# Kernel3 of a Nystrom attention block: two passes of scores with tokens on partitions instead of one pass and transposes

## The chip, the cores and the metric

The kernel runs on one core of a Trainium2 chip. The metric is device time of one execution in microseconds (us). The core has a matrix engine (TensorE, in the profile PE, with its weight loads as PEld), a vector engine (DVE), a scalar engine (ACT), a general engine (POOL) and a queue for transfers (SP). PE writes its products to PSUM; the other engines read them from there.

## The reference

The input `x` is 16 batches of 1024 tokens by 256 features. A block of attention and a block of experts follow each other, each on normalized input, each added to its input after a second normalization. The attention, cut to what matters:

```python
H, M = (16, 64)                      # heads, landmarks; HD = 16
Q = Q / HD ** 0.5
Q_l = Q.reshape(b, H, M, n // M, HD).mean(axis=-2)     # one landmark for 16 tokens
K_l = K.reshape(b, H, M, n // M, HD).mean(axis=-2)
kernel1 = softmax(einsum('bhnd,bhmd->bhnm', Q, K_l), axis=-1)
kernel2 = softmax(einsum('bhmd,bhkd->bhmk', Q_l, K_l), axis=-1)
kernel3 = softmax(einsum('bhmd,bhnd->bhmn', Q_l, K), axis=-1)
SV = matmul(matmul(kernel1, iterative_inv(kernel2)), matmul(kernel3, V))
out = transpose(SV, (0, 2, 1, 3)).reshape(b, n, c) @ w_proj
```

`iterative_inv` is six rounds of four 64x64 products for each head. The second block computes eight expert reconstructions of every token, takes for each batch the expert of least loss, gathers that expert's adapter weights by its number, and adds the adapter's output to a base product. The change concerns `kernel3` and its product with `V` alone: for each head, 64 landmarks against 1024 tokens, a softmax over the tokens, and a sum of V over the tokens with these weights.

## The kernel before

All data is float32. Each batch passes four stages: `stage_a` (normalize, transpose, Q, K, V, landmarks, kernel3 and its product with V, called `u`), `stage_p` (kernel2 and its inverse, then the inverse times `u`, called `pw`), `stage_c` (kernel1, its product with `w_bd`, the projection) and `stage_d1`/`stage_d2` (experts, choice, gather, adapter). Four streams run through the batches at once, so that in the steady part PE works on stage a of one batch, p of the batch before and c and d of the ones before these. In the trace of batch 8's stage a, stage p works on batch 7, c on 6 and d on 5.

The order of instructions on PE, ACT, DVE and POOL is written out by the program. Every stage is a generator that yields a `go(name, follows, parts)` ahead of each piece of work: the parts are planned durations on the engines (`mm` for PE, with the mode of the array and the pool of PSUM; `ew` for the others), and a planner at the end of the file chooses the stream whose next piece can start first on PE, with its own clocks and its own model of the PSUM buffers. Engines then run their instructions strictly in that order. PSUM is one pool, `ps2`, of four buffers of two banks; every product tile takes the next of the four in turn, and must wait until the tile that had it before is read.

Kernel3 in stage a works in four steps, two groups of 8 heads (`c`) by two halves of 512 tokens (`n`):

- `scores` (L339 to L352): four products of 32 rows each (`psc`, landmarks of two heads on the 128 partitions, 512 tokens in the free direction) in two PSUM tiles; DVE takes the negated maximum of each row (`nmx`, L349), and ACT the exponential with that as bias and the row's sum as a second output (`e`, L352).
- `turned` (L368, L370): sixteen 128x128 transposes of `e`, so that tokens stand on partitions, and two copies by ACT back to SBUF (`e3t`).
- `times_v` (L379, L386): sixteen products, for each of four token blocks and four pairs of heads, with 32 columns of `v` as the stationary operand, and a copy (`ut`).

At the end the two halves, which have different maxima, are brought together (`share`, L430 to L438), four transposes turn `ut` back (`pu`, L443), and DVE scales and adds (`un`, `u`, L448 and L452).

Stage c does kernel1 in two passes: maxima first (`max_of`, L648 and L656), transposed to rows (L677, L679), then scores with a second product that subtracts the maximum (`weights`, L686 and L694, exponential L704), then products with 34 columns of `w_bd`, 17 for each head, of which the last is a column of ones that gives the sum (`weighted`, L715 to L726). Stage p's products are L491, with ACT's copies `kv` (L571), `sq` (L586), `vi` and `vt` (L609, L611) and DVE's `t1` (L574), `t2` (L584), `t3` (L595). Stage d has the hidden products `ph` (L833), the reconstructions `pr` (L865), DVE's difference (L873) and ACT's squares (L876), the choice of the expert (`row`, L905 to L914), five gathers by POOL (L917), and the output products `pad` (L945) and `pf` (L960, L961).

## Time and profile before

| what | value |
|---|---|
| median of 11 runs | 2829.7 us (2825.94 to 2833.56) |
| profiled execution, its own time | 2823.92 us |
| its span, first to last instruction | 2822.1 us |
| mean granted clock of TensorE | 0.922 |
| ACT: squares `df` (L876), exponentials `e` of kernel3 (L352), `e3t` copies (L370), exponentials of kernel1 (L704) | 362.8, 172.5, 125.1, 124.2 us busy |
| DVE: `df` (L873), maxima of kernel3 (L349), maxima of kernel1 (L656) | 299.6, 150.2, 149.4 us busy |
| PE: `pr` (L865), `ph` (L833), `pq` (L285), scores of kernel3 (L339) | 253.6, 239.4, 233.0, 76.5 us busy |
| time of the chain that ended last, by engine | PE 62%, DVE 16%, ACT 15%, issue 4% |

Busy time of a group is the union of its instructions' times. A float32 matmul is two matmul records and two weight loads in the trace, a transpose one of each. Matmuls overlap each other, so the time a group of them takes is better read from the start of the group to the start of the next one than from the sum of their durations. "Idle before" is time in which the engine stood still ahead of an instruction, with the instruction that ended the wait; "issue" stands where no semaphore explains it. In the list of groups the columns after the count are busy time in us, mean duration in ns, and idle time before in us with its releasers.

### The profile page before, as it was taken

The page shows a single profiled execution, that of the slowest core. Times are in us where ns is not written, and L with a number is a line of the kernel's source. Part 1 is how long each engine was busy: PE and PEld are TensorE (multiplying, and loading weights), DVE is VectorE, ACT ScalarE, POOL GpSimd, SP SyncE. Part 2 cuts the span into 40 slices and gives each one's busy share as a digit, 9 for nine tenths or more (in the row PEclk, how much of TensorE's full clock was granted, in tenths as well). Part 3 has the DMA queues.
Part 4 walks back from the last instruction along what each step waited for, and adds up shares of the span by engine and source line. Part 5 has one row for each costly group of instructions (what it writes and reads, how often), then busy time and mean ns, then how long its engine had stood idle before and what let it go on. Part 6 is the DMA issues. An engine that isn't in the chain of part 4 may idle for free.

```text
span 2822.1 us, 86591 instructions
## 1 busy us (share of the span) xinstructions
PE 2400.4 (85%) x39362; PEld 1597.8 (57%) x39362; DVE 1533.6 (54%) x3195; ACT 1396.7 (49%) x2707; POOL 419.9 (15%) x434
## 2 busy tenths in 40 slices
PE   6898979989798898988879888898888979887865
PEld 3566555655656556565565555656566555655542
DVE  4556545465554655546554564555546555464644
ACT  3555644545455463544635545354464545544434
POOL 0001020120301202011120211203012030111131
PEclk9999989989899898998989999898998989999988
DMA  3000010010100101001010010101001010010100
GB/s 94 17 17 18 2 34 17 4 46 2 33 17 4 46 2 34 17 4 46 4 32 17 12 39 4 32 17 30 20 4 46 2 34 2 4 32 4 32 18 17
DMA packets 56569, 60.38 MB, mean 21 GB/s; under 512 B 4949, under 2 KB 55178, under 8 KB 56202
## 3 DMA queue, kind: packets, MB, share of 16 engines
q1 hardware_dynamic: 50176, 50.34, 5.7%
q8 instruction: 309, 5.06, 0.7%
q0 software_dynamic: 2560, 2.14, 0.3%
q10 hardware_dynamic: 3466, 2.37, 0.3%
q14 instruction: 58, 0.48, 0.1%
HBM read 38.06 MB, written 16.78 MB: 19 GB/s over the span
## 4 chain that ended last, share of the span: by engine, by line
PE 62%; DVE 16%; ACT 15%; issue 4%; another core or an unknown queue 1%; ACTq 0%; DMA 0%; POOLq 0%; DVEq 0%; POOL 0%
PE pq L285 8%; PE ph L833 8%; PE pr L865 5%; ACT df L876 5%; ACT e L352 4%; PE pf L960 4%; PE pv L306 4%; PE pt L368 3%; DVE maxima L656 3%; PE pvi L491 3%; PE pkv L491 3%; PE put L379 2%; PE psv L715 2%; PE po L763 2%; DVE nmx L349 2%
## 5 line engine op out<-in xcount | busy, mean ns | idle before, releaser
L876 ACT ACTIVATE df<-df,bd_sb 128x512 f32<-128x512 f32 x512 | 362.8, 711 | 152.7 <-DVE df L873 152.7
L873 DVE TENSOR_TENSOR df<-pr,xt_d 128x1024 f32<-128x1024 f32 x256 | 299.6, 1217 | 104.3 <-PE pr L865 81.8
L352 ACT ACTIVATE e<-psc,nmx 128x512 f32<-128x512 f32 x256 | 172.5, 686 | 207.6 <-DVE nmx L349 175.9
L865 PE MATMUL pr<-ht,wd_sb 64*128 64x512 f32 x1024 | 253.6, 614 | 10.6 <-DVE maxima L656 5.2
L833 PE MATMUL ph<-xt_d,wd_sb 128*128 128x512 f32 x512 | 239.4, 610 | 2.1 <-DVE df L873 1.4
L198 POOL TENSOR_SCALAR ve_c_y<-mv_c_y 128x4 f32<-128x4 f32 x32 | 7.4, 230 | 1557.3 <-DVE mv_c_y L196 1497.3
L285 PE MATMUL pq<-xt_a,wqkv_sb 128*128 128x512 f32 x512 | 233.0, 600 | 0.0
L574 DVE SCALAR_TENSOR_TENSOR t<-pkv,eye 128x512 f32<-128x512 f32 x96 | 65.4, 682 | 221.3 <-ACT kv L571 221.3
L704 ACT ACTIVATE e<-psct 128x1024 f32<-128x1024 f32 x128 | 124.2, 1024 | 96.9 <-PE psct L694 96.9
L656 DVE TENSOR_REDUCE maxima<-psc 128x16 f32<-128x1024 f32 x128 | 149.4, 1218 | 36.2 <-PE psc L648 36.1
L491 PE MATMUL pkv<-vi,k2t 64*64 64x64 f32 x6144 | 125.4, 235 | 49.1 <-ACT vi L609 40.4
L285 PEld LDWEIGHTS pq<-xt_a,wqkv_sb 128*128 128x128 f32 x512 | 95.0, 191 | 116.9 <-issue 112.9
L491 PEld LDWEIGHTS pkv<-vi,k2t 64*64 64x64 f32 x6144 | 110.5, 147 | 88.3 <-ACT vi L609 45.7
L349 DVE TENSOR_REDUCE nmx<-psc 128x2 f32<-128x1024 f32 x128 | 150.2, 1214 | 17.6 <-PE psc L339 17.1
L833 PEld LDWEIGHTS ph<-xt_d,wd_sb 128*128 128x128 f32 x512 | 93.2, 192 | 113.7 <-issue 102.6
L368 PE MATMUL pt<-ident,e 128*128 128x128 f32 x1024 | 143.3, 298 | 11.8 <-ACT e L352 5.8
L865 PEld LDWEIGHTS pr<-ht,wd_sb 64*128 64x128 f32 x1024 | 88.3, 186 | 102.4 <-issue 58.7
L370 ACT COPY e3t<-pt 128x1024 f32<-128x1024 f32 x128 | 125.1, 1023 | 41.2 <-PE pt L368 40.9
L368 PEld LDWEIGHTS pt<-ident,e 128*128 128x128 f32 x1024 | 126.8, 154 | 21.1 <-ACT e L352 8.5
L960 PE MATMUL pf<-wbase_sb,xt_d 128*128 128x256 f32 x512 | 133.2, 382 | 0.0
L195 DVE BATCH_NORM_STATS2 st_d_y<-y_d 128x6 f32<-128x256 f32 x128 | 51.5, 403 | 148.9 <-ACT y_d L239 148.9
L648 PE MATMUL psc<-bd,qt 32*128 32x128 f32 x2048 | 95.6, 324 | 42.1 <-ACT e L352 38.1
(166 smaller groups left out, 4567.4 us busy)
## 6 DMA issues: line engine op xcount, KB each, us to landing
xa<-in_L_attn_x_dram SPq DMA_DIRECT2D x16, 1024.0 KB, 5.5
x<-in_L_attn_x_dram SPq DMA_DIRECT2D x16, 1024.0 KB, 7.6
out_dram<-y_d SPq DMA_DIRECT2D x32, 512.0 KB, 2.9
wqkv_sb<-in_L_attn_w_qkv_dram ACTq DMA_DIRECT2D x1, 768.0 KB, 6.4
wd_sb<-in_L_ffn_Wd_dram ACTq DMA_DIRECT2D x2, 256.0 KB, 12.8
wd_sb<-in_L_ffn_Wd_dram ACTq DMA_DIRECT2D x1, 512.0 KB, 14.1
wdn<-in_L_ffn_Wa_down_dram,row POOLq DMA_INDIRECT x32
wproj_sb<-in_L_attn_w_proj_dram ACTq DMA_DIRECT2D x1, 256.0 KB
```

The costliest lines, as they stand in the source:

```text
L285: nc.tensor.matmul(pq[:, n, :], lhsT=wqkv_sb[:, k, f0 : f0 + P], rhs=xt[:, k, n * 512 : (n + 1) * 512], start=(k == 0), stop=(k == NC - 1),)
L349: nc.vector.tensor_reduce(nmx[:, n, q : q + 2], psc[g], X, ALU.max, negate=True)
L352: nc.scalar.activation(e3[:, i, :], psc[g][:, i, :], AF.Exp, bias=nmx[:, n, q + i : q + i + 1], accum_out=s3[:, n, q + i : q + i + 1],)
L368: nc.tensor.transpose(pt[:, t, i, :], e3s[g][:, i, t * P : (t + 1) * P], ident)
L370: nc.scalar.copy(e3t, pt)
L491: nc.tensor.matmul(dst[64 * h[to] : 64 * h[to] + 64, 4 * h[frm] + 2 * g0 + g1, :], lhsT=x[rows, i, :], rhs=y[rows, j, :] if y_at else y[ro ...
L656: nc.vector.tensor_reduce(mx[:, t0 : t0 + 2, 64 * g : 64 * g + 64].rearrange("x t (p j) -> x p t j", p=2)[:, :, :, 0 : 2 * NC], psc[g].rea ...
L833: nc.tensor.matmul(ph[:, n, :], lhsT=wd1_sb[:, k, 2 * i : 2 * i + 2, :].rearrange("p e h -> p (e h)"), rhs=xt[:, k, n * 512 : (n + 1) * 51 ...
L865: nc.tensor.matmul(pr[:, r, :], lhsT=wd2_sb[half, i, k * P : (k + 1) * P], rhs=ht[half, cols], start=True, stop=True,)
L873: nc.vector.tensor_tensor(df, pr, middle(xt[:, k, cols], 2), ALU.subtract)
L876: nc.scalar.activation(df[:, r, :], df[:, r, :], AF.Square, bias=bd2_sb[:, e, k : k + 1], accum_out=part[:, e, k * NW + n : k * NW + n + 1],)
L960: nc.tensor.matmul(po[:, j, :], lhsT=xt[:, k, cols], rhs=wbase_sb[:, k, :], start=(k == 0), stop=False)
```

## The change

Kernel3 takes the form that kernel1 has, with its sides exchanged. In a first pass the same score products as before are made for all four steps (`max_of`, new L360), and DVE takes only their maxima. The maxima of the two halves are joined (`maxima3`), transposed by one PE transpose (`pm`), and multiplied with a picking matrix into `mrow`, which holds the negative maxima as rows. The second pass (`weights`) has four steps of 256 tokens: four products of `ones` with `mrow` put the negative maximum in every place of a PSUM tile, sixteen products of 128 tokens of `kt` (stationary) with `bd` add the scores, now with tokens on partitions, and ACT takes one exponential over 1024 columns, without bias or sum. `times_v` multiplies these weights, 32 landmarks at a time, with 34 columns of `v_ones`: V with a column of ones beside the 16 of each head, so that the sum over the tokens comes out of the same product. 64 such products of 128 tokens by 32 by 34 make one step; the steps are added in `sums` by one ACT copy and three DVE additions, and at the end DVE divides. The transposes of `e`, the `e3t` copies, `share`, `pu` and `un` are gone. ACT's copy of V now writes into `v_ones` with a gap of one column for each head; the ones are set once by POOL. The planned durations and the order follow: all four steps of the first pass are yielded ahead of the second pass, and the next batch's normalization is yielded after the second step of it. In the changed order of batch 8's neighbourhood, PE has `pr` x4, `pkv3`, three steps of maxima, `psq3`, `psct`, `pb3`, the fourth step of maxima, `psv`, `pvi3`, `psct`, `pkv4`, the transpose of the maxima, `psv`, `psq4`, and then the weights, with `pad`, `pf` and stage p's products between them; the last two V groups stand side by side.

```diff
--- before.py
+++ after.py
@@ -161,6 +161,14 @@
 
 
 
+
+    v_ones = const.tile([P, NT, H, HD + 1], F32, name="v_ones")
+    nc.gpsimd.memset(v_ones.rearrange("p t h d -> p (t h d)"), 1.0)
+
+    maxima3 = const.tile([P, 4, 32], F32, name="maxima3")
+    nc.gpsimd.memset(maxima3, 0.0)
+    minus_pick = const.tile([P, NC], F32, name="minus_pick")
+    nc.vector.tensor_reduce(minus_pick, ident.rearrange("x (p j) -> x j p", j=32)[:, 0:NC, :], X, ALU.add, negate=True)
     w_bds = [const.tile([P, NP, 2, HD + 1], F32, name=f"w_bd{i}") for i in range(2)]
     maxima = [const.tile([P, 4, P], F32, name=f"maxima{i}") for i in range(2)]
     for t in (*w_bds, *maxima):
@@ -262,7 +270,6 @@
             load(b + 1, "xa", 1)
         both = [("a", b, "xt", h) for h in range(NW)]
         qt = kt = None
-        v = work.tile([P, NT, D], F32, tag="v", name=f"v_{b}", bufs=1)
         lsum = small.tile([P, 2, NC, M], F32, tag="lsum", name=f"lsum_{b}", bufs=1)
         for i, scale in enumerate((HD**-0.5, 1.0)):
             for c in range(NC):
@@ -310,7 +317,9 @@
                         start=(k == 0),
                         stop=(k == NC - 1),
                     )
-            nc.scalar.copy(v[:, t0 : t0 + 4, :], pv)
+            nc.scalar.copy(
+                v_ones[:, t0 : t0 + 4, :, 0:HD], pv.rearrange("p j (h d) -> p j h d", d=HD)
+            )
             if t0 == 0:
                 yield go(
                     ("a", b, "bd"),
...
+        mx3 = small.tile([P, NW, NP], F32, tag="mx3", name=f"mx3_{b}")
+        sums = small.tile([P, NP, 2 * (HD + 1)], F32, tag="sums3", name=f"sums3_{b}", bufs=1)
+        TC = 2
+        steps = range(NT // TC)
+
+        def before_max(c, n):
+            return go(
+                ("a", b, "max", c, n),
+                [("a", b, "bd"), ("a", b, "qk", 1, c)],
+                mm(0.5, "r32", "ps2"),
+                mm(0.5, "r32", "ps2"),
+                ew("dve", 1.22, 1, "free"),
+                ew("dve", 1.22, 1, "free"),
+            )
+
+        def max_of(c, n):
+            psc = [two_banks([P, 2, 512], f"psm3_{b}_{c}_{n}_{g}") for g in range(PC // 2)]
             for p in range(PC):
                 nc.tensor.matmul(
                     psc[p // 2][:, p % 2, :],
@@ -343,113 +364,111 @@
                     start=True,
                     stop=True,
                 )
-            e3s = []
             for g in range(PC // 2):
                 q = c * PC + 2 * g
-                nc.vector.tensor_reduce(nmx[:, n, q : q + 2], psc[g], X, ALU.max, negate=True)
-                e3 = buf4k("e3", [P, 2, 512], f"e3_{b}_{c}_{n}_{g}")
-                for i in range(2):
-                    nc.scalar.activation(
-                        e3[:, i, :],
-                        psc[g][:, i, :],
-                        AF.Exp,
-                        bias=nmx[:, n, q + i : q + i + 1],
-                        accum_out=s3[:, n, q + i : q + i + 1],
-                    )
-                e3s.append(e3)
-            return e3s
-
-        def turned(c, n, e3s):
-            e3ts = []
+                nc.vector.tensor_reduce(mx3[:, n, q : q + 2], psc[g], X, ALU.max)
+
+        def before_weights(i):
+            return go(
+                ("a", b, "e3", i),
+                [("a", b, "mrow")],
+                mm(1.15, "r32", "ps2"),
+                mm(1.15, "r32", "ps2"),
+                ew("act", 1.03, 1, "free"),
+                ew("act", 1.03, 1, "free"),
+            )
+
+        def weights(i):
+            psc = [two_banks([P, 2, TC, NC, P], f"psc3_{b}_{i}_{g}") for g in range(PC // 2)]
+            for p in range(PC):
+                nc.tensor.matmul(
+                    psc[p // 2][:, p % 2].rearrange("x t c l -> x (t c l)"),
+                    lhsT=ones[rows32(p), :],
+                    rhs=middle(mrow[rows32(p), :, :].rearrange("x c l -> x (c l)"), TC),
+                    start=True,
+                    stop=False,
+                )
+            for c in range(NC):
+                for t in range(TC):
+                    cols = slice((TC * i + t) * P, (TC * i + t + 1) * P)
+                    for p in range(PC):
+                        nc.tensor.matmul(
+                            psc[p // 2][:, p % 2, t, c, :],
+                            lhsT=kt[rows32(p), c, cols],
+                            rhs=bd[rows32(p), c, :, :].rearrange("f r l -> f (r l)"),
+                            start=False,
+                            stop=(c == NC - 1 and t == TC - 1),
+                        )
+            es = []
             for g in range(PC // 2):
-                pt = two_banks([P, 4, 2, P], f"pt3_{b}_{c}_{n}_{g}")
-                for t in range(4):
-                    for i in range(2):
-                        nc.tensor.transpose(pt[:, t, i, :], e3s[g][:, i, t * P : (t + 1) * P], ident)
-                e3t = buf4k("e3t", [P, 4, 2, P], f"e3t_{b}_{c}_{n}_{g}")
-                nc.scalar.copy(e3t, pt)
-                e3ts.append(e3t)
-            return e3ts
-
-        def times_v(c, n, e3ts):
-            put = one_bank([P, P], f"put_{b}_{c}_{n}")
-            for t in range(4):
-                for p in range(PC):
+                e = buf4k("e3", [P, 2, TC, NC, P], f"e3_{b}_{i}_{g}", 4)
+                nc.scalar.activation(e, psc[g], AF.Exp)
+                es.append(e)
+            return es
+
+        def before_values(i):
+            return go(
+                ("a", b, "ut", i),
+                [("a", b, "e3", i), *(("a", b, "v", h) for h in range(NW))],
+                mm(1.5, "c32", "ps2"),
+                ew("act" if i == 0 else "dve", 0.4, -1, "free"),
+            )
+
+        def times_v(i, es):
+            put = one_bank([P, NP, 2 * (HD + 1)], f"put_{b}_{i}")
+            for p in range(PC):
+                for c in range(NC):
                     q = c * PC + p
-                    nc.tensor.matmul(
-                        put[rows32(p), :],
-                        lhsT=v[:, 4 * n + t, q * 32 : q * 32 + 32],
-                        rhs=e3ts[p // 2][:, t, p % 2, :],
-                        start=(t == 0),
-                        stop=(t == 3),
-                    )
-            nc.scalar.copy(ut[:, n, c, :], put)
-
...
         ahead = norm_a(b + 1) if b + 1 < NB else iter(())
-        yield before_scores(*steps[0])
-        e3s = scores(*steps[0])
-        for i, step in enumerate(steps):
-            yield go(
-                ("a", b, "e3t", *step),
-                [("a", b, "e3", *step)],
-                mm(0.88, "full", "ps2"),
-                mm(0.88, "full", "ps2"),
-                ew("act", 1.03, 0, "free"),
-                ew("act", 1.03, 1, "free"),
-            )
-            e3ts = turned(*step, e3s)
-            if i + 1 < len(steps):
-                yield before_scores(*steps[i + 1])
-                e3s = scores(*steps[i + 1])
+        for n in range(NW):
+            for c in range(NC):
+                yield before_max(c, n)
+                max_of(c, n)
+        yield go(
+            ("a", b, "mcol"), [("a", b, "max", c, n) for c in range(NC) for n in range(NW)], ew("dve", 0.15, None)
+        )
+        nc.vector.tensor_tensor(
+            maxima3[:, :, 0:NC],
+            *(mx3[:, n, :].rearrange("x (c p) -> x p c", c=NC) for n in range(NW)),
+            ALU.max,
+        )
+        yield go(("a", b, "mrow"), [("a", b, "mcol")], mm(0.15, "full", "ps2"), ew("dve", 0.4, -1, "free"))
+        pm = one_bank([P, P], f"pm3_{b}")
+        nc.tensor.transpose(pm, maxima3.rearrange("x p j -> x (p j)"), ident)
+        mrow = small.tile([P, NC, P], F32, tag="lsum", name=f"mrow_{b}", bufs=1)
+        nc.vector.tensor_tensor(mrow, middle(pm, NC), last(minus_pick, P), ALU.mult)
+        e3s = {}
+        for i in steps:
+            yield before_weights(i)
+            e3s[i] = weights(i)
             if i == 1:
                 yield from ahead
-            yield go(
-                ("a", b, "ut", *step),
-                [("a", b, "e3t", *step), *(("a", b, "v", h) for h in range(NW))],
-                mm(1.0, "c32", "ps2"),
-                ew("act", 0.25, -1, "free"),
-            )
-            times_v(*step, e3ts)
-        uts = [("a", b, "ut", *step) for step in steps]
-        yield go(("a", b, "share"), uts, ew("dve", 0.5, None), ew("act", 0.25), ew("dve", 0.6))
-
-        least = small.tile([P, NP], F32, tag="nml", name=f"nml_{b}", bufs=1)
-        nc.vector.tensor_tensor(least, nmx[:, 0, :], nmx[:, 1, :], ALU.min)
-        share = small.tile([P, NW, NP], F32, tag="share", name=f"share_{b}", bufs=1)
-        nc.vector.tensor_tensor(share, middle(least, NW), nmx, ALU.subtract)
-        nc.scalar.activation(share, share, AF.Exp)
-        nc.vector.tensor_tensor(s3, s3, share, ALU.mult)
-        rs3 = small.tile([P, NP], F32, tag="rs3", name=f"rs3_{b}")
-        nc.vector.tensor_tensor(rs3, s3[:, 0, :], s3[:, 1, :], ALU.add)
-        nc.vector.reciprocal(rs3, rs3)
-        nc.vector.tensor_tensor(share, share, middle(rs3, NW), ALU.mult)
-        yield go(("a", b, "u"), [("a", b, "share")], mm(0.44, "full", "ps2"), ew("dve", 0.8, -1, "free"))
-        pu = one_bank([P, NW, NP, 2 * HD], f"pu_{b}")
-        for n in range(NW):
-            for c in range(NC):
-                nc.tensor.transpose(
-                    pu[:, n, c * PC : (c + 1) * PC, :].rearrange("p q d -> p (q d)"), ut[:, n, c, :], ident
-                )
-        un = small.tile([P, NW, NP, HD], F32, tag="lsum", name=f"un_{b}", bufs=1)
+            if i > 0:
+                yield before_values(i - 1)
+                times_v(i - 1, e3s.pop(i - 1))
+        yield before_values(steps[-1])
+        times_v(steps[-1], e3s.pop(steps[-1]))
+        yield go(("a", b, "u"), [("a", b, "ut", i) for i in steps], ew("dve", 0.9, None))
+        by_head = sums.rearrange("x q (r d) -> x q r d", r=2)
+        rs3 = small.tile([P, NP, 2], F32, tag="rs3", name=f"rs3_{b}", bufs=1)
+        nc.vector.reciprocal(rs3, by_head[:, :, :, HD])
+        u = small.tile([P, NP, HD], F32, tag="u", name=f"u_{b}")
         for r, half in halves():
-            nc.vector.tensor_tensor(
-                un[half], pu[half, :, :, r * HD : (r + 1) * HD], last(share[half], HD), ALU.mult
-            )
-        u = small.tile([P, NP, HD], F32, tag="u", name=f"u_{b}")
-        nc.vector.tensor_tensor(u, un[:, 0], un[:, 1], ALU.add)
+            nc.vector.tensor_tensor(u[half], by_head[half, :, r, 0:HD], last(rs3[half, :, r], HD), ALU.mult)
         live[b]["u"] = u
 
 
```

## The prediction

> **What bounds the kernel now.** I read the page's busy table and its slices first, then the groups by line with shapes kept apart, then the PE timeline of one steady batch, then sums over windows of it.
>
> ```profile
> span 2822.1 us, 86591 instructions
> PE 2400.4 (85%) x39362; PEld 1597.8 (57%) x39362; DVE 1533.6 (54%) x3195; ACT 1396.7 (49%) x2707; POOL 419.9 (15%) x434
> PEclk9999989989899898998989999898998989999988
> ```
>
> PE is the bound (85%); ACT and DVE are half idle, so work taken off ACT alone is worth nothing. PEclk gives the granted clock in 40 slices, in tenths of full speed (9 is 90% or more), and several show 8: there is lost clock to win or lose.
>
> In the timeline the first `ph` of a batch starts at 1138.8, 1312.8, 1485.9 and 1657.6: a period of 173 us, repeated from about 450 to 2350 us. The 90 us in which batch 8 goes through kernel3:
>
> ```profile
> 1046.30:1136.30 90.00, 70.30 (x1263) 53.29 (x1262) 54.98 (x143) 38.97 (x74) 26.18 (x26) 0.87 0.09 27
> 1097.70:1108.00 10.30, 7.46 (x160) 6.35 (x164) 9.86 (x37) 4.97 (x12) 6.26 (x7) 0.50 0.20 69
> 1138.80:1312.80 174.00, 151.28 (x2465) 101.23 (x2461) 95.33 (x199) 87.24 (x169) 26.20 (x26) 0.91 0.07 21
> ```
>
> Columns are length, busy time of PE, PEld, DVE, ACT and POOL, then the granted clock. PE idles 90.00-70.30 = 19.7 us in this stretch, against 22.7 in a whole period: nearly all of PE's idle time lies where kernel3 is worked. The clock falls to 0.50 in four pieces of it (6.8, 10.3, 3.4 and 3.4 us, with 5.33+7.46+3.40+3.40 = 19.6 us of busy PE), which costs 9.8 us, since that work would take half as long. The idle time before some groups there (in brackets, with its releaser):
>
> ```profile
> 1095.28 0.69 PE L491 MATMUL pvi<-t,vt 64*64 64x64 f32 x32 [1.62 <-DVE t L595]
> ...
> 1099.78 1.99 PE L491 MATMUL pkv<-vi,k2t 64*64 64x64 f32 x64 [3.34 <-ACT vi L609]
> ...
> 1119.67 0.49 PE L648 MATMUL psc<-bd,qt 32*128 32x128 f32 x4 [2.26 <-ACT e L352]
> ...
> 1131.68 3.64 PE L226 MATMUL pt_d<-ident,xn_d 128*128 128x128 f32 x16 [3.77 <-DVE k L524]
> ```
>
> The second and third are kernel3's doing: ACT holds `vi` behind four exponentials that wait for DVE's maxima, and PE's next scores wait for buffers that the exponentials still read.
>
> **The change on PE, per batch.** These rows price what goes and what comes:
>
> ```profile
> L368 PE MATMUL pt<-ident,e 128*128 128x128 f32 x1024 | 143.3, 298 | 11.8 <-ACT e L352 5.8 <-ACT e L704 5.8
> L379 PE MATMUL put<-e3t,v 128*32 128x128 f32 x2048 | 101.2, 343 | 10.4 <-issue 7.5 <-ACT e L352 2.4 <-ACT e3t L370 0.4
> L648 PE MATMUL psc<-bd,qt 32*128 32x128 f32 x2048 | 95.6, 324 | 42.1 <-ACT e L352 38.1 <-DVE cmx L544 2.0 <-DVE svn L726 1.7
> L694 PE MATMUL psct<-mt,minus_max 32*128 32x512 f32 x512 | 84.1, 609 | 0.0
> L715 PE MATMUL psv<-w_bd,e 128*32 128x34 f32 x8192 | 99.0, 208 | 23.3 <-issue 18.0 <-DVE t L595 2.5 <-ACT e L352 1.5
> ```
>
> Removed are 4 groups of 16 transposes (L368), 4 of 16 products with V (L379) and the four `pu` transposes. The score products stay as the first pass. Added are 4 times: four products of `ones` with `mrow` (shape of L694), sixteen of `kt` with `bd` (shape of L648) and 64 products of weights with `v_ones` (shape of L715); and one transpose. Busy times (each group over 64, times 4): removed (143.3+101.2+9.9)/16 = 15.9 us, added (84.1+95.6+99.0)/16+0.3 = 17.7, so +1.8. From a group's start to the next group's start in the timeline, medians: transposes 1.87, V products 1.71, `pu` 0.44; L694 0.97, L648 1.29, L715 1.97: 14.8 out, 17.1 in, +2.3. I take +2.1: **PE gets more work, not less**.
>
> A rule that speaks against the change: the Trainium skill, "TensorE: Matmul & The Clock Gate", section "Wait — 56ns, not 53.3ns?", says that starts of matmuls never come closer than about 25 ns however few columns they stream. L715's 128 records start within 1.32 us (median), 10 ns apart, so the row decides; by the page a V group would be an estimated 3.2 us and the sum 75 us higher.
>
> **ACT and DVE.** ACT loses 16 exponentials with their accumulator reads (two start 1.33 us apart in the timeline: 10.7 us) and 8 copies of 0.97; it gains 8 exponentials of 1024 (L704, 1.02). Some 10 us less per batch, in an engine with room: worth only what waits in front of PE (below). DVE keeps its 8 maxima (1.17 apart); `share` and `un` go (2.4 us), three sums (0.4 each), `mrow`, `u` and small ones come (2.6): nothing. The memset of `v_ones` on POOL (2176 columns; L167 takes 0.49 for 512, so 2.1 us) is covered by 8.3 us in which POOL waits for the first statistics; without that cover it costs 2 us once. No DMA moves.
>
> **PE's waits, per batch.** The order of the changed program is known; I walk it with the durations above from the start of `pkv3` (time 0). Ahead of it stand four `pr` groups with no `po` between them, so ACT is busy with their squares until 5.3, `kv` ends at 5.8 and DVE's `t1` at 6.4; DVE's next six instructions are maxima (to 13.4). PE issues `pkv3`, three max groups, `psq3` and `psct`; every one of the four buffers then waits for one DVE maximum: 7.0, 7.6, 8.8, 9.9, 11.1, 12.3. The fourth max group ends at 16.5, with 8.8 us of PE work done: 7.7 idle. Behind it `psct` waits for the last two maxima, which DVE reaches after `row` (20.7): 2.0, and `psv` for its exponentials: 0.7. Together 10.4. From there to the end of the next `psc1` (75) I find nothing over 0.3: the exponentials wait for no maximum any more, `pkv5` has a V group in front of it, and `pt_d` comes behind a `pq` of 3.6 us, so the four waits shown above go.
>
> Instruction supply: PE waits put down to "issue" are 3.7 us of the 19.7 (3.3 around the five gathers of L917, 1060 to 1067, 0.45 after a `psv`), and stay. Four more groups of 256 PE instructions (128 loads, 128 matmuls) come; in the trace PE's fetches of 256 never follow each other in under 3.4 us, and a `psv` group uses 256 in 1.3. L715's 18.0 us and the 8.8 before `pkv`, over 64 groups, are 0.4 each: 1.7 for four, less 0.5 that L379 had; the last two V groups stand back to back and may wait up to 2 more. I take +2.0, bounds 0 and 4.
> The Trainium skill, "Runtime: NRT & Kernel Launch", "Instruction fetch mechanics", holds that the fetch of these blocks of 256 is hidden; the 0.45 and 1.5 us stalls behind `psv` disagree, and by the page the 2.0 would be 0.
>
> So idle: 10.4+3.7+2.0 = 16.1 for 19.7: -3.6, bounds -8 (DVE reaches the maxima earlier) and +2 (it reaches them later).
>
> Clock: it fell in before where PE was busy for under about half of some 3.4 us. The walk has one such place for certain (3.8 to 13), with work at half clock until about 24, partly inside the waits. I take 7.5 us lost for 9.8: -2.3, bounds 4 and 13 us lost.
>
> **Sum:** 2.1-3.6-2.3 = -3.8 us per batch; the first batch runs alone, so 15 of them: **-57 us**. On the profiled execution: span 2822.1, 2765 after (1.8 us lie around it); the runs' median is 5.8 above that execution's 2823.9, so 2829.7-57 = **2773 us**.
>
> **Rivals.**
> *Slower: the burst of maxima.* For it: six maxima in a row on DVE with PE's four buffers behind them, and an order made with PE costs lower than the rows (a V group planned at 1.5, row 1.97). If the idle there is 12 us and half clock then lasts into the weights (13 us lost), the batch is 2.1-2.0+3.2 = +3.3 us: 2880. It decides from 11.3 us lost on, where the sum passes zero. Against it: the pieces shown above lose 9.8 already.
> *A larger gain.* If the maxima are reached early and the clock stays up (idle 12.7, lost 4.5): 2.1-7.0-5.3 = -10.2, 2677. For it: all waits on L352 go (38.1 us before L648 alone). Against it: DVE's queue in order.
> *No change to speak of.* More work and fewer waits cancel, within 0.4 us per batch: 2824 to 2835. 0.2% (6 us) is about what a measurement of this kernel can tell from none.
>
> **How the numbers follow.** Forecast, 2715 to 2824: 0.40; larger gain: 0.15; no change: 0.07; slower: 0.38. Faster is thus 0.55. The range holds the forecast, half of the slower cases and part of the larger gain: 2700 to 2880. The likeliest's own range is 2715 to 2824.
>
> **What would show it.** The V groups near 1.5 us busy and the two products of the weights near 1.3 and 1.5; PE busy up by some 30 us less what the clock gives back; PE waits on the maxima of kernel3 near 10 us per batch and none on its exponentials; period near 169 us. I am wrong if the V groups cost over 2.5 us, if PE waits for instructions by over 4 us more per batch, or if the granted clock falls below 0.90.

## The result and the profile after

The changed kernel takes 2865.93 us (median of 8 runs, 2844.86 to 2874.28) against 2830.25 for the kernel before (30 runs): a ratio of **1.0122, 95% interval 1.0108 to 1.0137**. It is slower by 1.2%, where a gain of 2% was forecast. The time lies in the range, on the wrong side of zero.

Of the profiled execution after, from the page: span, busy engines, granted clock in 40 slices and the queue that brings PE its instructions (packets, MB, share). The last fence has that queue's line of the kernel before.

```profile
span 2865.9 us, 101087 instructions
...
PE 2486.1 (87%) x46994; PEld 1608.5 (56%) x46994; DVE 1532.7 (53%) x3180; ACT 1216.6 (42%) x2131; POOL 420.7 (15%) x436
...
PEclk9999989999898998989989898998989989899988
...
q8 instruction: 368, 6.03, 0.9%
```

```profile
q8 instruction: 309, 5.06, 0.7%
```

ACT lost 180 us of busy time and DVE kept its own, as foretold. The mean granted clock is 0.923, as before (0.922). PE is busy for 85.7 us more, with 46,994 matmuls and as many loads where it had 39,362 of each. The queue brings 59 packets more (368 for 309). Each has 16,384 bytes; taken as 256 instructions they make 15,104, which fits what the trace counts: PE's loads and matmuls grew by 15,264, all its instructions by 15,140.

The sums over windows of it, in the form of those shown before: the stretch of one batch from its third `pkv` on, and a whole period.

```profile
1231.50:1309.00 77.50, 66.75 (x1397) 45.15 (x1396) 40.11 (x100) 27.80 (x44) 19.96 (x20) 0.85 0.10 31
1164.90:1342.00 177.10, 157.56 (x2939) 101.95 (x2938) 94.69 (x198) 75.92 (x133) 26.00 (x26) 0.91 0.07 21
```

The period is 177 us (before 173, forecast 169). PE idles 19.5 us of it, against 22.7, and the granted clock in it is 0.91, as before.

The waits of PE: which group, for whom, us in total, times, longest. First the kernel before, then the changed one.

```profile
PE pvi L491 <- DVE t L595: 56.7, 27, 6.1
PE pt_d L226 <- DVE k L524: 42.4, 11, 4.2
PE pkv L491 <- ACT vi L609: 40.4, 14, 3.3
PE psc L648 <- ACT e L352: 38.1, 25, 2.3
PE pvi L491 <- issue: 23.4, 46, 1.2
...
PE psv L715 <- issue: 18.0, 21, 1.7
...
PE pkv L491 <- issue: 8.8, 8, 1.9
PE put L379 <- issue: 7.5, 13, 1.0
```

```profile
PE put L424 <- issue: 43.5, 24, 2.4
PE psv L734 <- issue: 39.5, 42, 2.3
PE pvi L510 <- issue: 39.0, 78, 1.3
PE psm L360 <- DVE t L593: 27.0, 11, 2.5
PE pkv L510 <- issue: 26.9, 16, 2.1
PE pb L510 <- issue: 24.8, 15, 2.1
...
PE pw L638 <- issue: 15.2, 8, 2.2
```

The first four rows of before, 178 us, are the four waits that the prediction shows. In the whole list after they are 6 us together. What leads it now is "issue": time in which no semaphore holds PE and no instruction comes. It was 64.0 us in all and is 207.1; the waits for semaphores went from 339 to 154.

The 43.8 us by which the span grew fall into four parts. "Lost to half clock" is half of PE's busy time inside the stretches of half clock (336.7 us before, 351.1 after); "work" is the rest of the busy time. The column "predicted" has the prediction's terms per batch, times 15.

| PE, whole run, us | predicted | measured |
|---|---|---|
| waits for semaphores (19.7 less 3.7 kept, to 10.4 per batch) | -84 | -185.0 |
| waits for instructions ("issue") | +30 | +143.1 |
| work at full clock | +32 | +78.5 |
| lost to half clock | -35 | +7.2 |
| sum | -57 | +43.8 |

The first term was better than foretold; the other three ate it, the second above all. With the second as forecast (+30) and the others as measured the sum would be -69, near the forecast: the errors of the other three nearly cancel, in part because waiting turned into work, in part by luck. How the second looks in the trace: PE's timeline, with start, duration and, in brackets, idle time before.

```profile
1288.84 1.30 PE L424 MATMUL put<-v_ones,e 128*32 128x34 f32 x128
1290.07 0.80 PE L510 MATMUL pkv<-vi,k2t 64*64 64x64 f32 x37
1292.63 0.68 PE L510 MATMUL pkv<-vi,k2t 64*64 64x64 f32 x27 [1.76 <-issue]
...
1308.73 1.54 PE L424 MATMUL put<-v_ones,e 128*32 128x34 f32 x156
1312.57 1.06 PE L424 MATMUL put<-v_ones,e 128*32 128x34 f32 x100 [2.31 <-issue]
1313.57 0.99 PE L638 MATMUL pw<-u,vt 64*64 64x16 f32 x28
1316.59 0.40 PE L638 MATMUL pw<-u,vt 64*64 64x16 f32 x4 [2.03 <-issue]
```

A V group of 256 instructions passes in 1.23 us. 37 records into the next group PE stands still for 1.76 us. The two V groups that stand side by side stop after 156 of their 256 matmuls, and the product behind them stops again. In the whole trace the fetches of 256 instructions never start closer than 3.3 us to each other, and 106 of them are closer than 4 us (37 before).

That PE waits for these fetches can be read from when the stalls end. Of the 85 stalls of over 1 us that are put down to issue, 78 end 1.1 to 1.6 us after a fetch has landed. Only 7% of all points in time lie so, and only 3 of the 43 waits of that length for semaphores end so. Counted at every length, such stalls are 30 us before and 154 us after: **123 of the 143 us**. The rest is 34 us before and 53 after, in short stalls, most of them while the gathers' transfers run (32 and 45 us, against none on the chip of run 6); what holds PE in those is not shown.

The groups of kernel3, shapes kept apart: count, then busy us, mean ns, idle before. First the score products of the kernel before, then the changed kernel's groups: L360 stands against L339, and L384, L395 and L424 against L694, L648 and L715 of the prediction.

```profile
L339 PE MATMUL psc<-kt,bd 32*128 32x512 f32 x512 | 76.5, 640 | 1.3 <-DVE df L873 0.7 <-DVE t L595 0.5
```

```profile
L360 PE MATMUL psm<-kt,bd 32*128 32x512 f32 x512 | 140.5, 781 | 31.7 <-DVE t L593 27.0 <-ACT vt L630 2.3 <-DVE df L892 1.3
...
L424 PE MATMUL put<-v_ones,e 128*32 128x34 f32 x8192 | 86.8, 199 | 43.8 <-issue 43.5
L384 PE MATMUL psc<-mrow,ones 32*128 32x512 f32 x512 | 81.7, 672 | 5.0 <-issue 4.4 <-DVE mrow L453 0.6
L395 PE MATMUL psc<-bd,kt 32*128 32x128 f32 x2048 | 80.9, 287 | 4.7 <-issue 4.7
```

The new products are cheaper than the rows they were priced by (81.7, 80.9 and 86.8 us for 84.1, 95.6 and 99.0). The score products that were to stay as they are are not: 140.5 us for 76.5. Why, one batch's timeline shows:

```profile
1231.54 1.16 PE L510 MATMUL pkv<-vi,k2t 64*64 64x64 f32 x64
1232.63 3.30 PE L360 MATMUL psm<-kt,bd 32*128 32x512 f32 x12
1238.39 4.34 PE L360 MATMUL psm<-kt,bd 32*128 32x512 f32 x12 [2.45 <-DVE t L593]
1242.66 1.13 PE L510 MATMUL psq<-kv 64*64 64x64 f32 x32
...
1248.62 2.04 PE L360 MATMUL psm<-kt,bd 32*128 32x512 f32 x8
1250.60 1.14 PE L734 MATMUL psv<-w_bd,e 128*32 128x34 f32 x109
1252.12 0.28 PE L734 MATMUL psv<-w_bd,e 128*32 128x34 f32 x6 [0.39 <-issue]
1252.89 0.27 PE L734 MATMUL psv<-w_bd,e 128*32 128x34 f32 x5 [0.49 <-issue]
```

This is the walk of the prediction. From `pkv3` to the end of the last maxima group it takes 19 us (16.5 foretold), but only 2.45 of them are idle. The tiles come free one at a time: in the trace two products of a group start together where four did before. And the clock is halved from 1237.2 to 1247.4: PE is "busy" for 4.34 us with twelve records that take 3.3 at the start of the burst. Behind it the five gathers run, and `psv` goes on in pieces of two to six records, one every 0.75 us.

### The profile page after: what moved, and what is told of

It reads as the page before. It is cut to its first block, busy times and chain, and to the rows that moved or that the text cites. A ratio compares the mean times of both kernels' runs of the same rounds, so it can differ in the third digit from the quotient of the medians.

```text
span 2865.9 us, 101087 instructions
## 1 busy us (share of the span) xinstructions
PE 2486.1 (87%) x46994; PEld 1608.5 (56%) x46994; DVE 1532.7 (53%) x3180; ACT 1216.6 (42%) x2131; POOL 420.7 (15%) x436
## 4 chain that ended last, share of the span: by engine, by line
PE 70%; DVE 10%; ACT 9%; issue 9%; ACTq 0%; DMA 0%; another core or an unknown queue 0%; POOLq 0%; POOL 0%; DVEq 0%
PE ph L852 8%; PE pq L292 7%; ACT df L895 5%; PE pv L313 4%; PE pf L979 4%; PE po L782 4%; PE pr L884 4%; PE pvi L510 4%; PE psct L705 3%; PE psv L734 3%; PE put L424 3%; PE psm L360 3%; PE psc L384 3%; PE pkv L510 2%; PE psct L713 2%
## 5 line engine op out<-in xcount | busy, mean ns | idle before, releaser
L405 ACT ACTIVATE e<-psc 128x1024 f32<-128x1024 f32 x128 | 124.1, 1021 | 148.8 <-PE psc L395 148.6
L360 PE MATMUL psm<-kt,bd 32*128 32x512 f32 x512 | 140.5, 781 | 31.7 <-DVE t L593 27.0
L203 DVE BATCH_NORM_STATS2 st_c_y<-y_c 128x6 f32<-128x256 f32 x128 | 51.5, 403 | 198.5 <-ACT y_c L247 198.5
L614 DVE TENSOR_TENSOR t<-pb,t 128x512 f32<-128x512 f32 x96 | 66.0, 687 | 167.5 <-PE pb L510 167.2
L369 DVE TENSOR_REDUCE mx<-psm 128x2 f32<-128x1024 f32 x128 | 147.9, 1215 | 9.4 <-PE psm L360 9.4
L734 PE MATMUL psv<-w_bd,e 128*32 128x34 f32 x8192 | 98.2, 201 | 43.6 <-issue 39.5
L424 PE MATMUL put<-v_ones,e 128*32 128x34 f32 x8192 | 86.8, 199 | 43.8 <-issue 43.5
```

The source lines that it names most:

```text
L360: nc.tensor.matmul(psc[p // 2][:, p % 2, :], lhsT=bd[rows32(p), c, :, :].rearrange("f r l -> f (r l)"), rhs=kt[rows32(p), c, n * 512 : (n ...
L369: nc.vector.tensor_reduce(mx3[:, n, q : q + 2], psc[g], X, ALU.max)
L424: nc.tensor.matmul(put[rows32(g), q, :], lhsT=es[p // 2][:, p % 2, t, c, 32 * g : 32 * g + 32], rhs=v_ones[:, TC * i + t, 2 * q : 2 * q + ...
L734: nc.tensor.matmul(psv[rows32(g), j // 2, col : col + 2 * (HD + 1)], lhsT=es[p // 2][:, p % 2, j * P + 32 * g : j * P + 32 * g + 32], rhs= ...
```

## The experiments

The kernels went to several chips, which differ: the kernel before takes 2830 us on the first, 2825 on that of runs 13 and 14 (whether the two are one chip is not on record), and 2746 to 2748 on three others. Each ratio is to the kernel before on the same chip.

**1. More instructions, same streaming.** In the kernel before, the moving side of each V product is cut into four: as many records as the changed kernel's V groups have, with the same columns in all.

```diff
@@ times_v of the kernel before
+                    for g in range(4):
                         nc.tensor.matmul(
-                            put[rows32(p), :],
+                            put[rows32(p), rows32(g)],
                             lhsT=v[:, 4 * n + t, q * 32 : q * 32 + 32],
-                            rhs=e3ts[p // 2][:, t, p % 2, :],
+                            rhs=e3ts[p // 2][:, t, p % 2, rows32(g)],
```

> The kernel before, with each of the V products (L379) split into four of 32 moving columns: same sums, 64 instead of 16 products in a group, 192 more PE instructions in each of 64 groups (12,288 in all). Theory 1 (PE waits for instructions): the change added 15,140 PE instructions and 143 us of PE idle time put down to issue (64 to 207), so this adds about 116 us of it, and the time goes from 2830 to 2890 or more. Rival (the burst of maxima and the half clock behind it cost the time): there is no such burst here, only the V groups' own time rises, from 1.71 to about 1.97 us as L715 has, 17 us: about 2847, not over 2860.

Measured: 2822.24 us, ratio 1.0279 [1.0256, 1.0302]; issue 55.7 us. Slower, but not for the reason on trial, as its V group's row shows:

```profile
L380 PE MATMUL put<-e3t,v 128*32 128x32 f32 x8192 | 195.6, 207 | 10.2 <-issue 6.8 <-ACT e L352 3.3
```

195.6 us busy against 101.2: the four neighbours write to the same 32 rows of the tile and follow each other (3.0 us from a group to the next, 1.7 before), so the instructions are spread over more time. The expectation on issue is missed. The time is higher than either theory needs, and since the edit changed the overlap too, the run decides nothing.

**2 and 3. The changed kernel's V products, wider.** 32 landmarks at a time become 64 or 128: half or a quarter of the V products, the same result.

```diff
@@ times_v of the changed kernel, 64 wide
-                        for g in range(4):
+                        for g in range(2):
                             nc.tensor.matmul(
-                                put[rows32(g), q, :],
-                                lhsT=es[p // 2][:, p % 2, t, c, 32 * g : 32 * g + 32],
+                                put[64 * g : 64 * g + 64, q, :],
+                                lhsT=es[p // 2][:, p % 2, t, c, 64 * g : 64 * g + 64],
```

> The changed kernel, with 64 instead of 32 landmarks as the stationary operand of the V products: 32 instead of 64 products in a group, 8,192 PE instructions fewer in all, the same sums and the same order. Theory 1: issue waits fall from 207 us to about 130, the V groups' own time rises by 0.3 to 0.5 us each (20 to 30 us): about 2815, between 2795 and 2835. Rival (burst of maxima): the burst is as before, so no gain: 2866 to 2895.

> The changed kernel, with all 128 rows of a pair of heads as the stationary operand: 16 products in a group, 12,288 PE instructions fewer in all. A load of 128 columns sets the pace (16 transposes took 1.75 us at best, so 32 records 3.5 us): a V group takes 1.5 us more than now, 97 us in all. Theory 1: issue waits fall to about 90 us, and the time is about 2866-116+97 = 2847. Rival: no wait goes, 2866+97 = 2963.

Measured: 64 wide 2662.05 us, **0.9684 [0.9660, 0.9709]**; 128 wide 2873.43, 1.0452 [1.0430, 1.0474]. The V rows, 64 wide first, then 128:

```profile
L424 PE MATMUL put<-v_ones,e 128*64 128x34 f32 x4096 | 129.9, 225 | 0.7 <-issue 0.3 <-ACT e L405 0.2
```

```profile
L424 PE MATMUL put<-v_ones,e 128*128 128x34 f32 x2048 | 287.6, 308 | 0.2 <-ACT e L405 0.2
```

At 64 the gain is larger than the theory had it (2815 for 2830 is 0.995). The wait for instructions is gone from the group, and the two groups side by side run through:

```profile
1218.24 3.93 PE L424 MATMUL put<-v_ones,e 128*64 128x34 f32 x128
1222.10 1.11 PE L638 MATMUL pw<-u,vt 64*64 64x16 f32 x32
```

Issue is 52 and 51 us, so both take most of the suspected cost away. At 128 the time is still that of the rival (2963 for 2830 is 1.047): V alone is busy for 287.6 us, 158 more than at 64 and 201 more than at 32 (the expectation had 97), and 511 us of the span run at half clock. The changed kernel itself was not run on this chip; on the others it has 1.007 to 1.012. That one change of width turns this into 0.968, with the burst of maxima in place (L360 is busy for 140.9 us), says that the instructions of V cost more than the whole difference between the kernels.

**4. Own columns only.** As 2, but with 17 columns for each half in place of 34, so half of the sums: `rhs=v_ones[:, TC * i + t, 2 * q + g, :]`.

> As the run with 64 landmarks, but each head's 64 landmarks are multiplied with the 17 columns of their own head alone (half of the 34 were never used), so PSUM, the sums and the division are half as large. Theory 1: as that run, or up to 20 us less: 2795 to 2830. Rival: 2866 to 2885.

Measured: 2673.48 us, 0.9730 [0.9709, 0.9751]; issue 49.5. Streaming half the columns gains nothing over run 2 (V is busy for 129.8 us, there 129.9), so the products are not bound by columns at this size. Why it is slightly slower (276 us at half clock against 225) was not settled.

**5 and 6. Both kernels as they are, on a chip of the faster kind.** No edit.

> The kernel before, unchanged, profiled on the chip of this call. Both theories: the times of its runs on this chip. If instruction supply differs between chips (theory 1: it does, since the run with split V products was compared with a kernel before of 2748 us instead of 2830), its issue waits on PE, 64 us in the first profile, are lower on a chip where it is faster, and above all those around the gathers; by the rival they are 64 us again and the difference lies in the granted clock alone.

> The changed kernel, unchanged, on the chip of this call. Theory 1: where the kernel before takes about 2750 us, stalls around the gathers are small on this chip for both, so the change costs less here than 1.2%: 0.99 to 1.01. Rival (the burst of maxima, the same on every chip): the ratio is 1.012 again.

Measured: before 2748.32 us (one run), after 2764.05, 1.0073 [1.0051, 1.0096]. Issue 30.4 and 154.2 us: +124, against +143 on the first chip. PE is busy for 57.6 us more and waits for semaphores 167 us less (328 to 160). The clock's part is the only one with another sign: half of the work at half clock is 142.2 us before and 132.4 after. And here next to all issue time ends 1.1 to 1.6 us after a fetch has landed: 29 of 29 us before, 154 of 154 after. Against run 2, on another chip of this kind, the changed kernel takes 102 us more, and its issue time is 102 us more (154.2 against 52.2); the V groups' 43 us more at 64 wide are paid for by 94 us less of work at half clock, which saves 47.

**7 and 8. Without the gathers.** On the first chip some of the issue time lies under the five gathers (33 us before, 47 after, counting stalls with a packet of theirs in the six microseconds before the stall's end). These kernels take expert 0's rows with plain transfers; the chosen expert is left out.

```diff
@@ gather in stage d of either kernel
+            r0 = P if col == 1 else 0
+            nc.gpsimd.dma_start(out=dst, in_=src[r0 : r0 + dst.shape[0], :])
```

> The kernel before, with the five gathers of each batch by expert number (L917) replaced by plain transfers of expert 0's rows: the chosen expert is left out of the result, the transfers stay. Theory 1: PE waits for instructions while gathers run, 3.3 us per batch on the first chip, so up to 50 us go where those stalls are, and next to nothing where they are not. Rival: no change within 10 us.

> The changed kernel with the same replacement: the chosen expert is left out. Theory 1: the stretch of psv and pvi3 under the gathers, 9.7 us for 2.4 us of work on the first chip, shrinks; the gain is larger than in the kernel before, by up to 4 us per batch (60 us). Rival: no more than in the kernel before.

Measured: before 2740.88 us, 0.9977 [0.9961, 0.9993], issue 31.9; after 2772.27, 1.0090 [1.0068, 1.0112], issue 161.4. The kernel before gains 0.2%, the changed one nothing. But on this chip there was little to gain: with the gathers the issue time ahead of `pvi` is 12.6 us in the changed kernel, where the first chip has 39.4, and in the kernel before there is none, where the first chip has 23.4. The gathers' part was not tried on a chip that has those stalls.

**9. The rival: spread the burst of maxima.** The planner is told that each maximum costs 2.4 us of DVE, so that it puts other work between the groups.

```diff
@@ before_max
-                ew("dve", 1.22, 1, "free"),
-                ew("dve", 1.22, 1, "free"),
+                ew("dve", 2.4, 1, "free"),
+                ew("dve", 2.4, 1, "free"),
```

> The changed kernel with the planned time of a first-pass maximum doubled (1.22 to 2.4 us), so that the planner puts other streams' work between the max groups: nowhere more than two groups in a row, instead of three and then a fourth close behind. PE instructions are the same in number. Theory 1 (instruction supply): issue waits stay near 150 us where the kernel before takes 2747 us (207 where it takes 2830), and the ratio to the kernel before falls by no more than 0.005 (1.002 to 1.010 where the changed kernel has 1.007). Rival (burst of maxima): the max groups' busy time falls from 140 to about 90 us and the half clock behind them goes, 50 to 80 us: 0.98 to 0.99.

Measured: 2795.26 us, 1.0181 [1.0154, 1.0208], slower than the changed kernel as it is and outside both expectations. The maxima groups, and the waits of PE:

```profile
L360 PE MATMUL psm<-kt,bd 32*128 32x512 f32 x512 | 131.8, 806 | 35.0 <-DVE t L593 21.6 <-DVE df L892 12.5 <-DVE mx L369 0.8
```

```profile
PE put L424 <- issue: 51.9, 30, 2.4
PE psc L384 <- DVE svn L745: 27.1, 10, 3.4
PE pq L292 <- DVE maxima L675: 25.3, 10, 2.6
```

Issue fell to 97.3 us, which the theory of supply had not expected, since it fell with the instructions unchanged; V's own share rose. In its place new waits for DVE came (the second and third row), idle time rose to 350 us and half clock to 407. The maxima groups are still busy for 131.8 us, where the rival wanted about 90: this order did not take the burst's cost away, so the run says nothing of what the burst costs, only that this order is no way out of it.

**10 and 11. Kernel1's products wider too.** `weighted` (L715, L734 after) has the same shape and got the same edit: 64 rows of `psv` at a time, in the kernel before and in the one of run 2.

```diff
@@ weighted of either kernel
-                    for g in range(4):
+                    for g in range(2):
                         nc.tensor.matmul(
-                            psv[rows32(g), j // 2, col : col + 2 * (HD + 1)],
-                            lhsT=es[p // 2][:, p % 2, j * P + 32 * g : j * P + 32 * g + 32],
+                            psv[64 * g : 64 * g + 64, j // 2, col : col + 2 * (HD + 1)],
+                            lhsT=es[p // 2][:, p % 2, j * P + 64 * g : j * P + 64 * g + 64],
```

> The kernel before, with 64 instead of 32 tokens as the stationary operand of kernel1's weighted products (L715): 8,192 PE instructions fewer. Theory 1: the kernel before starves little (30 to 64 us of issue waits, 26 of them at psv and the pkv behind it), and the wider groups take about 0.3 us more each (19 us), so little is left: 0.990 to 1.002. Rival: no change or up to 0.7% slower.

> The changed kernel with 64-wide stationary operands in both its V products and kernel1's weighted products: 16,384 PE instructions fewer than the changed kernel has, fewer than the kernel before. Theory 1: issue waits fall from 52 us (V products alone) to about 20, against 20 us more of PE work: 0.960 to 0.972, about what the V products alone gave (0.968). Rival: over 1.0.

Measured: on the kernel before 2747.27 us, 1.0007 [0.9996, 1.0018]; on run 2's 2642.09, **0.9624 [0.9603, 0.9646]**, the best version. Of the latter, the page and its two groups:

```profile
span 2640.4 us, 84707 instructions
...
PE 2451.6 (93%) x38802; PEld 1622.0 (61%) x38802; DVE 1553.1 (59%) x3180; ACT 1216.2 (46%) x2131; POOL 421.1 (16%) x436
```

```profile
L734 PE MATMUL psv<-w_bd,e 128*64 128x34 f32 x4096 | 138.2, 228 | 6.0 <-ACT e L723 5.5 <-DVE mx L369 0.4
L424 PE MATMUL put<-v_ones,e 128*64 128x34 f32 x4096 | 129.3, 225 | 0.2 <-ACT e L405 0.2
```

Issue is 0.4 and 0.2 us: with both widened, PE never waits for instructions worth naming. In the kernel before that is worth nothing: PE is busy for 40 us more than in run 5, which takes up the 30 us of issue. Both expectations of run 10 allow its result. With kernel1 wide on both sides the change is worth 2642.09 for 2747.27, again 0.962. PE is busy for 93% of the best version.

**12. The best version, spread.** As 9, on the kernel of run 11.

> Both edits together: 64-wide stationary operands in V and weighted products, and the planned time of a first-pass maximum doubled. Theory 1 with the burst as a second, smaller cost: 0.945 to 0.965. If the burst of maxima costs nothing once instructions come in time: as without it, 0.960 to 0.972.

Measured: 2762.39 us, 1.0065 [1.0048, 1.0082]; issue 0.3, idle 263.7, half clock 324 us for 223. This is outside both expectations: with supply out of the way, this order costs 120 us. The maxima groups are busy for 130.2 us, for 139.1 in run 11, so here too the burst's cost stays, and what it is worth remains open.

**13. Run 1 again, with strips that change.** The same cuts as in run 1, with the pairs of heads (`p`) innermost, so that neighbours write to different rows of the tile.

```diff
@@ times_v of the kernel before, against run 1
             for t in range(4):
-                for p in range(PC):
-                    for g in range(4):
+                for g in range(4):
+                    for p in range(PC):
```

> The kernel before with each V product split into four of 32 moving columns, as in the first split run, but with the four column strips of the array in the innermost loop, so that neighbouring products can overlap as before: 12,288 PE instructions more, work of a V group at most that of L715 (1.2 to 1.3 us for 128 records when nothing is late). Theory 1 (supply of instructions): issue waits on PE rise from 30 us to 100 or more where the kernel before takes 2747 us, and the time is 1.015 to 1.035 of it. Rival (the first split run was slow because its products shared a strip, and instructions cost nothing): issue stays below 60 us, at most 17 us more in all, 1.000 to 1.006.

Measured: 2878.06 us against 2825.49, **1.0190 [1.0171, 1.0208]**. Its V and `psv` rows:

```profile
L380 PE MATMUL put<-e3t,v 128*32 128x32 f32 x8192 | 106.2, 216 | 22.8 <-issue 18.9 <-ACT e L352 3.3 <-ACT e3t L370 0.4
L716 PE MATMUL psv<-w_bd,e 128*32 128x34 f32 x8192 | 100.9, 208 | 38.8 <-issue 35.3 <-DVE t L596 2.3 <-ACT e L705 1.2
```

V is busy for 106.2 us (101.2 before), so streaming and overlap are as they were; what differs is 12,288 PE instructions. Against the profile of the kernel before that the prediction reads (from the first chip), they cost 45.8 us: issue 64.0 to 107.6 (+43.6), busy +26.6, semaphores -24.4. The rival, that instructions alone are nearly free, falls. Issue rose by less than was expected (and this chip is not of the kind that the expectation takes). The rest of the price shows as busy time, about half of it lost to half clock (12.7 us).

**14. The changed kernel on that chip.** No edit.

> The changed kernel again, on the same chip, as the measure for the run beside it: 1.005 to 1.013 of the kernel before, issue waits on PE of 150 us or more.

Measured: 2855.40 us, 1.0102 [1.0082, 1.0123]; issue 189.9. The result repeats there.

## Why the prediction was wrong

*PE's waits: right, and too careful.* The four waits that were to go went, and next to nothing waits for kernel3's exponentials (0.2 us before L424). The walk gave 10.4 us of waits per batch; semaphores hold PE for 154 us in the whole run after, with 27 of them before the maxima groups. Part of what it called waiting is counted as work, at half clock, in these groups.

*Instruction supply: the step that failed.* "I take +2.0, bounds 0 and 4." Measured is +143 us over 15 batches, **9.5 per batch**. The prediction had seen that fetches of 256 come no closer than 3.4 us (one pair in that trace is at 3.3) and that a V group uses 256 in 1.3, and then priced the group by the average stall of `psv` (0.4 us), as if stalls added up singly. In the kernel before, the dense groups stand apart, with slow work between them in which the fetches catch up. After, V, `pkv`, `pb`, `psc` and `pw`, all dense, follow each other, and each group uses up the instructions that were fetched ahead for the next: half of the new stalls are not at V at all, but at `pkv`, `pb`, `pvi` and `pw`, none of which the change touched. The stalls end with the fetches (123 of the 143 us), and runs 2 and 11 show what they are worth: with fewer instructions for the same products the change gives 0.968 and 0.962. Run 13 shows it from the other side: the instructions without the change cost 1.9%.

*PE's work: mis-sized, +32 for +78.5.* Two errors. The maxima groups were taken as unchanged and cost 64 us more of busy time. By the time from each record to the next start it is 67: 42 because their tiles come free singly, and 25 because 51 us of them fall into half clock. And the removed groups were priced by rows that held half clock (34.5 us of the transposes' time and 56.3 of V's lie in it), while the clock's gain was counted as a term of its own: some of that gain was counted twice. The new products were priced too high, by 29 us, which hides part of it.

*The clock: wrong, -35 for +7.* The stretches of half clock are 443.0 us long in both kernels. The rule that it was forecast by does not carry over: in the trace before, PE was busy for less than half of the 3.4 us ahead of 64 of the 72 falls, in the trace after ahead of 29 of 59. Where most of the stalls are gone half clock does shrink, to 224 us in run 2 (about 380 before and 330 after on the chip of runs 5 and 6).

*The rivals.* The slower one named the right sign, and the burst does cost what the paragraph on PE's work says; but run 2 shows that the kernel wins with the burst in it, so it is not what turns the sign. What it would gain without the burst no run shows, since the order of runs 9 and 12 left the burst's cost in place. The larger gain (2677 us for 2830, 5.4%) was not reached; run 11 got 3.8% once supply was out of the way. Of the three signs that were to show the forecast wrong, V's price (1.36 us) and the clock (0.923) did not come; "PE waits for instructions by over 4 us more per batch" did.

The Trainium skill's "Runtime: NRT & Kernel Launch", section "Instruction fetch mechanics", which holds that the fetch is hidden, would have the supply at nothing; the 154 us of stalls that end with a fetch disagree. "TensorE: Matmul & The Clock Gate", "Wait — 56ns, not 53.3ns?", with its 25 ns from start to start, would have made a V group an estimated 3.2 us. The group took 1.23, so the row decided rightly; but the speed that this section rules out is what outruns the fetches.

*Open.* Why the kernel before takes 2825 to 2830 us on some chips and 2746 to 2748 on three, with short stalls around the gathers on the former alone; what the burst of maxima is worth; how much of the added busy time is work stretched by late instructions; why spreading lowers the issue time.

## What to carry to other kernels

Count PE's instructions per microsecond beside its time: here 256 of them want 3.3 us, and a stretch of small products that uses them faster runs on what was fetched ahead, and then stops, often in the next group. When such a product can be made wider at some cost in busy time, try the widths between: of the three here, the best is the first whose instructions come in time (32 wide 256 instructions in 1.2 us with stalls, 64 wide 128 in 2.0 with none, 128 wide 64 in 3.7). A wait that is removed is worth what the next limit leaves, so price that limit for the order after, not by its average in the order before.

## What the runs showed of the hardware

- Fetches of PE's instructions (16 KB, 256 by the count above, about 1 us in the queue) start at least 3.2 us apart in every trace here, however long PE waits for them, and a stall for them ends 1.1 to 1.6 us after one has landed. 256 in 3.3 us makes an estimated 77 PE instructions per us over a dense stretch; the most in any 20 us of the trace after is 80 per us, in any 5 us 125.
- A product of 34 moving columns for 128 tokens has a price by its stationary width: groups of the same work take 1.23, 1.99 and 3.7 us from start to next at 32, 64 and 128 wide, and half the moving columns at 64 gained nothing.
- Neighbouring products into the same 32 rows of a tile follow each other (3.0 us for a group of run 1), into different ones they overlap (1.7 us for the same products in run 13).
- One kernel differs by 3% between chips, more than the whole effect under study, while the ratios of two kernels agree to half a per cent (1.012, 1.007, 1.010).
